# A four-layer graph network on one core: a written-out order for layer 2, and attention heads on quarters of the TensorE array

## The chip, the cores and the metric

The kernel runs on one core of a Trainium2 chip. The metric is the device time of one execution in microseconds; the kernel before takes 2139.83 us, the median of three runs (2136.4 to 2140.26). A profiled execution takes longer, 2252.29 us, and all times that come from the profile are on that longer scale.

## The reference, cut to what matters

Four graph layers run one after the other on x (8 batches, 2048 nodes, 64 features) with one sparse adjacency matrix of 2048 x 2048. Each is followed by x = layernorm(x + layer(x)). The change touches layers 2 and 3:

```python
# layer 2
agg = einsum('ij,bjf->bif', A, x) / maximum(deg, 1)
out = relu(x @ W_self + b_self + agg @ W_neigh + b_neigh)
out = layernorm(out) * ln_gamma + ln_beta
# layer 3: 4 heads, then one more attention over their result
h    = einsum('bnc,hdc->bhnd', x, Wh)
attn = softmax(where(mask, einsum('...nd,...md->...nm', h, h), NEG))
z    = leaky_relu(concat_heads(attn @ h + bh))
h2   = z @ Wo.T
out2 = leaky_relu(softmax(mask(h2 @ h2.T)) @ h2 + bo); out = layernorm(out2) * gamma + beta
```

## The kernel before, in words

**Tiles.** Nodes come in 16 tiles of 128 (NT), batches in four pairs (NP): a pair's two batches of 64 features fill 128 partitions once transposed. Each node tile has three lists of 128 gathered neighbours (GS) for each of four groups of 32 nodes (NG); a gather is one indirect DMA on GpSimd's queue (`gather`, L186) that brings 128 rows of 2 KB. Layers 1 and 2 compute the first nine node tiles (DENSE) with the matrix ET, transposed and held in SBUF, and the other seven with gathered lists.

**Layer 2, preparation.** For every tile X is transposed (`transposed`, L108), multiplied with W_self and W_neigh (L747), the neighbour part written to the table ytab (L752) and split into three bf16 pieces Y (L753 to L759), the self part put into S (L754), and beta added to X (L760). The weights of the heads are prepared in the same stretch: for each of the four heads Wh and Wo are loaded as block diagonals of two copies (L659, L660), and G = Wh' x Wh, AT and WoT are made from them (L663 to L670), two heads sharing a buffer.

**Layer 2, sums.** 144 steps (9 tiles x 16 blocks) of three matmuls each (L828) add up the matrix tiles; between them, at fixed spacing, the 21 quads of the list tiles (`add_edges`, L814: eight instructions on four strips of 32 columns of the array) and their gathers. `finish` follows a tile's last sum: scaling by 1/deg and adding S (L779), Relu on ScalarE (L780), and, when both of a pair of tiles (`mates`) are there, two layer norms with a product with gamma and the residual between them (L786, L787). A layer norm is four statistics instructions a tile on VectorE (L137), twelve small VectorE instructions for the inverse square root (L123 to L143), and eight ScalarE instructions a tile, one to a batch (L151). Then Xo, the copy of X whose feature 0 is a one, goes to the table xtab (L793). Tile 0 also runs `first_nodes`: scores of its nodes with themselves, from which the shift of the exponent is written into G, and the four sides U of tile 0. The order on each engine is made by the tile framework's scheduler here: it may move instructions of one engine ahead of others.

**Layer 3, heads.** Scores of nodes n and m for head h are x_n' G x_m. For each node tile, four groups of nodes times two parts of lists make eight steps, and the order of every engine is the order in the program (`tc.manual_schedule`). A step has: gathers six steps ahead (`fetch`); four PE transposes of a gathered tile to xsT (`turn`, L890) and ScalarE's copy (L892); `score` (L905), which multiplies each pair's two halves on two row halves of the array with the side U, then exp on ScalarE (L908) and the edge mask on VectorE (L914); and `back` (L931), which adds up weighted rows in po, on two column halves. Every second step po is copied to o (L936), which frees its only buffer. Into these steps the table `beside` puts the work of the tiles before and after: `load_nodes` and `turn_nodes` (x of the next tile, from xtab, transposed, L681), `side` (U = G x, L687, four heads), `sums` (the rows of ones turned into columns through a DRAM table, L948, and inverted, L949), `through_w` (AT x o, L953, Leaky Relu on ScalarE and VectorE, L956, L957), `through_wo` (z x WoT, L962, scaled by the inverted sums, L964, added up on GpSimd, L968) and `pieces` (three bf16 pieces for the last attention, L983 to L988). The products of `side`, `through_w` and `through_wo` use the whole 128 x 128 array with block-diagonal weights, half of which are zeros; their results go to PSUM tiles pm of one bank, of which there are two (f3psm). The second attention (fifth) follows and is not touched.

Instructions go to five engines with a queue each; a semaphore wait at the head of a queue holds everything behind it on that engine.

Of the kernel before, what the change touches and what calls it, by code (L numbers as in the profile page):

```python
# [48 lines left out]
def kernel(ctx: ExitStack, tc: tile.TileContext, ins: dict, out: bass.AP):  # L49
# [590 lines left out]
    ps_m = early.enter_context(tc.tile_pool(name="f3psm", bufs=2, space=PSUM))  # L640
# [5 lines left out]
    for Xo in ones_x:  # L646
        nc.gpsimd.memset(Xo[:, :, 0:1], 1.0)

# [3 lines left out]
    for h in range(HN):  # L652
        wb = hp.tile([P, P], F32, name=f"wb{h % 2}")
        nc.gpsimd.memset(wb, 0.0)
        ob = hp.tile([P, P], F32, name=f"ob{h % 2}")
        nc.gpsimd.memset(ob, 0.0)
        for k in range(2):
            half = slice(k * D, (k + 1) * D)
            nc.sync.dma_start(wb[half, half], ins["L3_gnn_Wh"][h])  # L659
            nc.sync.dma_start(ob[half, half], ins["L3_gnn_Wo"][:, h * D:(h + 1) * D])  # L660
            nc.vector.tensor_scalar(wb[half, half], wb[half, half], wb[half, k * D:k * D + 1], None, op0=ALU.subtract)
        pg = misc([P, P])
        nc.tensor.matmul(pg, wb, wb, start=True, stop=True)  # L663
        nc.vector.tensor_copy(G[:, h], pg)
        pw = misc([P, P])
        nc.tensor.transpose(pw, wb, ident)
        nc.vector.tensor_copy(AT[:, h], pw)
        pw = misc([P, P])
        nc.tensor.transpose(pw, ob, ident)
        nc.vector.tensor_copy(WoT[:, h], pw)  # L670
        for k in range(2):
            nc.sync.dma_start(AT[k * D:k * D + 1, h, k * D:(k + 1) * D], ins["L3_gnn_bh"][h:h + 1, :])
    Us, xTs = {}, {}
    mean_row = f3w.tile([P, P], F32, name="mean_row")
    nc.vector.memset(mean_row, 1.0 / (B * P))
    shift = f3w.tile([P, 1], F32, name="shift")

    def turn_nodes(it, xi):
        px = misc([P, NP, P])
        for p in range(NP):  # L680
            nc.tensor.transpose(px[:, p], xi[:, p * P:(p + 1) * P], ident)  # L681
        xTs[it] = hp.tile([P, NP * P], F32, name="xT", bufs=2)
        nc.scalar.copy(xTs[it], px.rearrange("p a n -> p (a n)"))

    def side(it, h):
        pu = misc([P, NP, P])
        nc.tensor.matmul(pu, G[:, h], xTs[it], start=True, stop=True)  # L687
        if h == 0:
            Us[it] = hp.tile([P, NP, HN, P], F32, name="U", bufs=2)
        if h % 2:  # L690
            nc.vector.tensor_copy(Us[it][:, :, h], pu)
        else:
            nc.scalar.copy(Us[it][:, :, h], pu)

    def first_nodes(xi):

        turn_nodes(0, xi)
        self_ = hp.tile([P, HN], F32, name="self_")
        for h in range(HN):
            pu = misc([P, NP * P])  # L700
            nc.tensor.matmul(pu, G[:, h], xTs[0], start=True, stop=True)
            sq = hp.tile([P, NP * P], F32, name="sq")
            nc.vector.scalar_tensor_tensor(sq, pu, 1.0, xTs[0], op0=ALU.mult, op1=ALU.mult, accum_out=self_[:, h:h + 1])
        pm = misc([P, HN])
        nc.tensor.matmul(pm, mean_row, self_, start=True, stop=True)
        nc.vector.tensor_scalar(self_, pm, -1.0, LEVEL, op0=ALU.mult, op1=ALU.add)
        for h in range(HN):
            for k in range(2):
                row = slice(k * D, k * D + 1)
                nc.vector.tensor_copy(G[row, h, row], self_[row, h:h + 1])  # L710
        for h in range(HN):
            side(0, h)

    with ExitStack() as l2:
        wp = l2.enter_context(tc.tile_pool(name="l2w", bufs=1))
        wk = l2.enter_context(tc.tile_pool(name="l2k", bufs=2))

# [9 lines left out]
        b2 = rows("b2", ins["L2_gnn_ln_beta"], wp)  # L727
        r_deg = wp.tile([P, NT], F32, name="r_deg")
# [34 lines left out]
        pa = l2.enter_context(tc.tile_pool(name="l2pa", bufs=3, space=PSUM))  # L763
        sums, rss, selfs, shown = {}, {}, {}, []

        mates = [(0, 1), (2, 3), (4, 5), (6, 7), (8,), (15, 14), (13, 12), (11, 10), (9,)]
        mate = {t: m for m in mates for t in m}

        def bank(it):
            m = mate[it]  # L770
            if it == m[0]:
                sums[m] = pa.tile([P, 2, B, D], F32, name="pa")
            return sums[m][:, m.index(it)]

        def finish(it):
            m = mate[it]
            po = sums[m][:, m.index(it)]
            zf = po.rearrange("p b d -> p (b d)")
            nc.vector.scalar_tensor_tensor(zf, zf, r_deg[:, it:it + 1], S[:, it].rearrange("p b d -> p (b d)"), op0=ALU.mult, op1=ALU.add)  # L779
            nc.scalar.activation(zf, zf, AF.Relu)  # L780
            if it != m[-1]:
                return
            zs = [sums[m][:, k] for k in range(len(m))]
            layer_norm(zs, wk)
            for t, z in zip(m, zs):
                nc.vector.tensor_tensor(z, z, over(g2, [P, B, D]), ALU.mult)  # L786
                nc.vector.tensor_tensor(X[:, t], z, X[:, t], ALU.add)  # L787
            layer_norm([X[:, t] for t in m], wk)
            for t in m:
                Xo = ones_x[len(shown) % len(ones_x)]  # L790
                shown.append(t)
                nc.scalar.copy(Xo[:, :, 1:], X[:, t, :, 1:])
                nc.sync.dma_start(xtab[t * P:(t + 1) * P, :], Xo.rearrange("p b d -> p (b d)"))  # L793
                if t == 0:
                    first_nodes(Xo.rearrange("p b d -> p (b d)"))

        quads = [(it, s) for it in by_list for s in range(GS)]

# [7 lines left out]
        def add_edges(n):  # L806
            it, s = quads[n]
            if s == 0:
                selfs[it] = wk.tile([P, GS, P], F32, name="self_")
                nc.scalar.activation(selfs[it], Sel[:, it], AF.Copy)  # L810
                sums[it] = bank(it)
            for g in range(NG):
                nodes = slice(g * GN, (g + 1) * GN)
                nc.tensor.matmul(sums[it][nodes].rearrange("p b d -> p (b d)"), selfs[it][:, s, nodes], rss[n][g],  # L814
                                 start=(s == 0), stop=(s == GS - 1))
# [3 lines left out]
        fetch(0)  # L819
        fetch(1)  # L820
        steps = [(it, jt) for it in by_matrix for jt in range(NT)]
        LATE, EARLY = 18, 10
        n = 0
        for k, (it, jt) in enumerate(steps):
            if jt == 0:
                sums[it] = bank(it)
            for q in range(3):
                nc.tensor.matmul(sums[it].rearrange("p b d -> p (b d)"), ET[:, jt, it * P:(it + 1) * P],  # L828
                                 Y[:, jt, q].rearrange("p a n -> p (a n)"), start=(jt == 0 and q == 0), stop=(jt == NT - 1 and q == 2))
            if jt == NT - 1:  # L830
                finish(it)
            while n < len(quads) and n * (len(steps) - LATE - EARLY) <= (k - LATE) * len(quads):
                add_edges(n)
                fetch(n + 2)
                n += 1
# [22 lines left out]
    with early, ExitStack() as heads:  # L858
# [5 lines left out]
        os, xss, xsTs, ws, pos, h2s, zs, dTs = ({} for _ in range(8))  # L864

        def load_nodes(it):
            xi = wk.tile([P, BD], F32, name="xi")
# [884 lines left out]
```

## Time and profile before

| what | from the profile of the kernel before |
|---|---|
| whole span | 2250.5 us, mean granted TensorE clock 0.775 |
| busy over the span | PE 1637.6, DVE 1390.5, ACT 997.3, POOL 1050.1 us |
| adjacency and layer 0 | 0 to about 530 us |
| layer 1 | to about 786 us |
| layer 2, preparation | 786 to 844 us |
| layer 2, sums and finishes | 844 to 1075 us, the first `turn` of the heads being at 1075.3 |
| heads | first steps to 1094, then evenly to 1785 us, last tile to about 1812 |
| second attention and checks | the rest |

PE is TensorE's matmuls, PEld its weight loads, DVE VectorE, ACT ScalarE, POOL GpSimd, SP the queue of the sync engine. Matmuls overlap in their pipeline, so a matmul's duration is longer than the time that it adds to a stream; that is read from the starts, or from the length of a run of them in the chain of waits. A float32 matmul appears as two instructions. The chain of waits follows the work back from the last instruction, at each step to what released it. The columns of a group are: line, engine, operation, what is written from what, shapes, count, busy us and mean ns of one, then the idle time just before it and what ended it.

### The profile page before, as it was taken

What the parts mean: (1) busy time and instruction counts of PE and PEld (TensorE: products, weight loads), DVE (VectorE), ACT (ScalarE), POOL (GpSimd) and SP (SyncE); (2) the same over time, 40 slices, a digit from 0 to 9 for tenths busy, and PEclk for the clock granted to TensorE, in tenths of its full rate; (3) what the DMA queues carried; (4) which work ended last, traced back from release to release, by engine and by line L of the source; (5) the groups of instructions that cost most, each with busy time, mean ns of one, the idle gap of its engine ahead of it and who ended that gap; (6) DMA issues with size and microseconds to landing.
All of it is one profiled execution on the core that took longest, in us unless ns stands there. A gap on an engine that the chain in (4) does not pass through costs nothing.

```text
span 2250.5 us, 33253 instructions
## 1 busy us (share of the span) xinstructions
PE 1637.6 (73%) x12259; PEld 909.4 (40%) x12294; DVE 1390.5 (62%) x2954; ACT 997.3 (44%) x2352; POOL 1050.1 (47%) x992
## 2 busy tenths in 40 slices
PE   3552445433899979862799998999899858878872
PEld 3541111111333363320677776777667612222220
DVE  6886587785655572435244444444444459999995
ACT  4542243438523252546344444444444324555555
POOL 0002666643645356430444444444434267777762
PEclk9855565566999999986799999999999955555555
DMA  7322666631278626441432233223322155555540
GB/s 196 134 98 82 180 183 182 182 112 57 94 264 301 221 85 177 131 123 42 123 93 81 85 101 103 74 89 101 106 70 84 54 155 161 151 157 161 160 135 21
DMA packets 127690, 287.47 MB, mean 128 GB/s; under 512 B 55680, under 2 KB 56192, under 8 KB 125440
## 3 DMA queue, kind: packets, MB, share of 16 engines
q0 software_dynamic: 64896, 217.10, 31.9%
q1 hardware_dynamic: 45984, 63.96, 8.5%
q10 hardware_dynamic: 16640, 4.20, 0.8%
q8 instruction: 99, 1.62, 0.3%
q14 instruction: 71, 0.58, 0.1%
HBM read 249.29 MB, written 35.91 MB: 127 GB/s over the span
## 4 chain that ended last, share of the span: by engine, by line
PE 39%; DVE 15%; ACT 7%; issue 7%; POOL 3%; DMA 2%; another core or an unknown queue 1%; SPq 0%; DVEq 0%; ACTq 0%; POOLq 0%
PE pscore L905 7%; PE pa L556 6%; PE po L931 5%; PE pt L890 5%; PE pm L953 3%; DVE pr L1078 3%; PE pa L828 3%; PE pm L687 2%; PE pm L962 2%; DVE w L914 2%; PE pa L608 2%; DVE st L137 2%; DVE sc L1083 2%; POOL hs L186 1%; ACT w L908 1%
## 5 line engine op out<-in xcount | busy, mean ns | idle before, releaser
L914 DVE SCALAR_TENSOR_TENSOR w<-w,Sel 128x512 f32<-128x512 f32 (+1 forms) x192 | 178.4, 956 | 257.9 <-ACT w L908 257.9
L186 POOL DMA_INDIRECT hs<-htab,src x192 | 183.8, 957 | 295.0 <-PE pe L408 203.7
L186 POOL DMA_INDIRECT xs<-xtab,src x192 | 200.1, 1042 | 133.5 <-DMA xtab<-Xo 63.4
L556 PE MATMUL pa<-R,ET 128*128 128x512 bf16 x841 | 197.0, 388 | 52.5 <-POOL R L544 34.2
L905 PEld LDWEIGHTS pscore<-U,xsT 64*128 64x128 f32 x3072 | 193.9, 198 | 82.2 <-issue 82.1
L151 ACT ACTIVATE X<-X,ln_m,ln_r 128x64 f32<-128x64 f32 x384 | 131.3, 427 | 204.2 <-DVE ln_m L143 75.0
L905 PE MATMUL pscore<-U,xsT 64*128 64x64 f32 (+1 forms) x3072 | 216.4, 290 | 0.0
L908 ACT ACTIVATE w<-pscore 128x1024 f32<-128x1024 f32 x128 | 131.0, 1024 | 191.0 <-PE pscore L905 126.2
L186 POOL DMA_INDIRECT hs<-ktab,src x192 | 186.3, 970 | 55.0 <-issue 47.7
L968 POOL TENSOR_TENSOR h<-h,h2h 128x512 f32<-128x512 f32 x48 | 60.9, 1269 | 270.8 <-DVE h2h L964 270.8
L1073 PE MATMUL pe<-hi,selTb 32*128 32x512 bf16 x576 | 138.8, 619 | 52.2 <-DVE pr L1078 27.9
L890 PE MATMUL pt<-ident,xs 128*128 128x128 f32 x768 | 132.7, 298 | 44.9 <-DMA xs<-xtab,src 37.1
L892 ACT COPY xsT<-pt 128x512 f32<-128x512 f32 x192 | 112.1, 584 | 117.5 <-PE pt L890 110.7
L931 PE MATMUL po<-w,xs 128*64 128x64 f32 (+1 forms) x3072 | 147.1, 246 | 17.6 <-DVE o L936 16.5
L556 PEld LDWEIGHTS <-ET 128*128 128x128 fp8e4 x864 | 84.4, 100 | 173.9 <-issue 82.7
L931 PEld LDWEIGHTS po<-w,xs 128*64 128x64 f32 x3072 | 122.0, 140 | 35.5 <-DVE o L936 18.7
L1078 DVE TENSOR_TENSOR pr<-pe,hs 128x1024 f32<-128x1024 f32 x96 | 116.9, 1217 | 15.0 <-DMA hs<-ktab,src 10.7
L186 POOL DMA_INDIRECT rs<-ytab,src x84 | 80.4, 957 | 82.6 <-PE pa L814 52.6
L1083 DVE TENSOR_REDUCE sc<-pr 128x16 f32<-128x1024 f32 x96 | 117.1, 1219 | 2.9
L828 PE MATMUL pa<-Y,ET 128*128 128x512 bf16 x420 | 102.0, 395 | 22.5 <-DVE X L787 12.6
L890 PEld LDWEIGHTS pt<-ident,xs 128*128 128x128 f32 x768 | 85.1, 147 | 72.5 <-issue 51.7
L1085 ACT ACTIVATE w<-sc,shift 128x16 f32<-128x16 f32 x96 | 29.3, 306 | 191.3 <-DVE sc L1083 146.5
(567 smaller groups left out, 3331.9 us busy)
## 6 DMA issues: line engine op xcount, KB each, us to landing
at<-in_adj SPq DMA_DIRECT2D x16, 1024.0 KB
rtab<-r SPq DMA_DIRECT2D x16, 512.0 KB
ptab<-hp SPq DMA_DIRECT2D x16, 384.0 KB
hi<-ptab SPq DMA_DIRECT2D x16, 384.0 KB
X<-in_x ACTq DMA_DIRECT2D x16, 256.0 KB
htab<-H SPq DMA_DIRECT2D x16, 256.0 KB
ytab<-y SPq DMA_DIRECT2D x16, 256.0 KB
xtab<-Xo SPq DMA_DIRECT2D x16, 256.0 KB
```

The costliest lines, as they stand in the source:

```text
L151: nc.scalar.activation(v[:, b], v[:, b], AF.Identity, scale=rstd[:, k:k + 1], bias=nmr[:, k:k + 1])
L186: nc.gpsimd.indirect_dma_start(out=dst, out_offset=None, in_=table[:, :], in_offset=bass.IndirectOffsetOnAxis(ap=src[:, it, s, g:g + 1], a ...
L556: nc.tensor.matmul(po[h].rearrange("p a f -> p (a f)"), ET[:, jt, it * P:(it + 1) * P], R[:, jt, q, h].rearrange("p a f -> p (a f)"), star ...
L828: nc.tensor.matmul(sums[it].rearrange("p b d -> p (b d)"), ET[:, jt, it * P:(it + 1) * P], Y[:, jt, q].rearrange("p a n -> p (a n)"), star ...
L890: nc.tensor.transpose(pt[:, p], xss[k][n][:, p * P:(p + 1) * P], ident)
L905: nc.tensor.matmul(pscore[:, k_, f0:f0 + HN * ni].rearrange("p (h i) -> p h i", i=ni), xsTs[k][t][half, p], Us[it][half, p, :, i0:i0 + ni] ...
L908: nc.scalar.activation(w.rearrange("p t k a h i -> p k t (a h i)"), pscore.rearrange("p k (t m) -> p k t m", t=n), AF.Exp)
L914: nc.vector.scalar_tensor_tensor(wt, wt, 3.0e38, edge, op0=ALU.min, op1=ALU.mult)
L931: nc.tensor.matmul(po[half, p, :, i0:i0 + ni], xss[k][t][:, f0:f0 + D], ws[k][:, t, k_, p], start=(s == 0 and p == 0), stop=(last and p == ...
L1073: nc.tensor.matmul(pe[:, k].rearrange("p b d -> p (b d)"), selTb[nodes, s * P:(s + 1) * P], hi[nodes, q], start=(q == 0), stop=(q == 2))
L1078: nc.vector.tensor_tensor(pr.rearrange("p k b d -> p (k b d)"), pes[u].rearrange("p k b d -> p (k b d)"), hss[u].rearrange("p k b d -> p ( ...
L1083: nc.vector.tensor_reduce(sc, pr, AX.X, ALU.add)
```

## The change

Four things are changed. In layer 2 the preparation of the heads' weights is moved out of the stretch ahead of the sums into it, as are the transposes of tile 0 and its scores (`beside` at steps 2 to 14, 64, 72 to 96 and 104), and the whole part is put under `tc.manual_schedule`, so that each engine's order is the program's. The finishes are gathered in batches of 2, 4, 4, 3, 1, 1 and 1 tiles in the order in which they end; Relu and the sum go to S in SBUF by VectorE, so that the PSUM sum is free after one instruction; the scaled z stands in two PSUM tiles of its own, and there are four sum tiles.

In the heads the products with G and with AT are made on four 64 x 64 quarters of the array, each with one non-zero block and two pairs of batches (`quarters`), so that no zeros are multiplied. Two of the quarters write to the other half of the partitions, so in pairs 2 and 3 the two batches change places; the table xtab holds these batches exchanged (three writes a tile), and `sums` and `through_wo` put them back. `through_wo` multiplies each half of z on its own row half with 64 columns instead of 128. The PSUM tile pm has two banks, one for each half, and there is one of it. `beside` gives at most one such product to each of two slots in a step, one ahead of the scores and one ahead of `back`. And x of the next tile comes from X in SBUF, with its rows of ones set by two memsets, instead of from the table.

```diff
+    def turn_nodes(it):
+        px = misc([P, NP, P])
+        for p in range(NP):
+            nc.tensor.transpose(px[:, p], X[:, it, 2 * p:2 * p + 2, :].rearrange("p b d -> p (b d)"), ident)
+        xTs[it] = hp.tile([P, NP * P], F32, name="xT", bufs=2)
+        nc.scalar.copy(xTs[it], px.rearrange("p a n -> p (a n)"))
+        for k in range(2):
+            nc.vector.memset(xTs[it][k * D:k * D + 1], 1.0)
...
-        pa = l2.enter_context(tc.tile_pool(name="l2pa", bufs=3, space=PSUM))
+        pa = l2.enter_context(tc.tile_pool(name="l2pa", bufs=4, space=PSUM))
+        pz = l2.enter_context(tc.tile_pool(name="l2pz", bufs=2, space=PSUM))
...
-        mates = [(0, 1), (2, 3), (4, 5), (6, 7), (8,), (15, 14), (13, 12), (11, 10), (9,)]
+        sizes = [2, 4, 4, 3, 1, 1, 1]
...
+            nc.vector.scalar_tensor_tensor(sf, sums.pop(it), r_deg[:, it:it + 1], sf, op0=ALU.mult, op1=ALU.add)
+            nc.vector.tensor_scalar(sf, sf, 0.0, None, op0=ALU.max)
...
+                pair_of = xtab[t * P:(t + 1) * P, BD // 2:].rearrange("n (a k d) -> n a k d", k=2, d=D)
+                for k_ in range(2):
+                    nc.sync.dma_start(pair_of[:, :, 1 - k_], Xo[:, B // 2 + k_::2])
...
+        beside = {**{2 + 4 * h: (prepare, h) for h in range(HN)}, 64: (turn_nodes, 0),
+                  **{72 + 8 * h: (own_scores, h) for h in range(HN)}, 104: (set_shifts,)}
...
+        with tc.manual_schedule(engines=engines):
+            fetch(0)
+            fetch(1)
...
+        ps_m = heads.enter_context(tc.tile_pool(name="f3psm", bufs=1, space=PSUM))
...
+            pq = misc2()
+            for k in range(2):
+                own = slice(k * D, (k + 1) * D)
+                for j in range(2):
+                    to = own if j == 0 else slice((1 - k) * D, (2 - k) * D)
+                    nc.tensor.matmul(pq[to, j, 0:2 * P], W[own, own], v[own, 2 * j:2 * j + 2].rearrange("p a n -> p (a n)"),
+                                     start=True, stop=True)
...
-                nc.tensor.matmul(ph[:, p], zs[it, h][:, p], WoT[:, h], start=True, stop=True)
+                for k in range(2):
+                    own = slice(k * D, (k + 1) * D)
+                    nc.tensor.matmul(ph[:, k, p * D:(p + 1) * D], zs[it, h][own, p], WoT[own, h, own], start=True, stop=True)
...
-            0: lambda it: [(load_nodes, it + 1)],
-            1: lambda it: [(through_w, it - 1, 0), (side, it + 1, 0)],
-            2: lambda it: [(sums, it - 1), (through_wo, it - 1, 0), (through_w, it - 1, 1)],
-            3: lambda it: [(through_wo, it - 1, 1), (through_w, it - 1, 2)],
-            4: lambda it: [(through_wo, it - 1, 2), (through_w, it - 1, 3)],
-            5: lambda it: [(through_wo, it - 1, 3), (side, it + 1, 1)],
-            6: lambda it: [(side, it + 1, 2), (side, it + 1, 3)],
-            7: lambda it: [(pieces, it - 1)],
+            0: lambda it: ([(turn_nodes, it + 1)], [(through_w, it - 1, 0)]),
+            1: lambda it: ([(side, it + 1, 0)], [(through_w, it - 1, 1)]),
+            2: lambda it: ([(sums, it - 1)], [(through_wo, it - 1, 0)]),
+            3: lambda it: ([(through_w, it - 1, 2)], [(through_wo, it - 1, 1)]),
+            4: lambda it: ([(side, it + 1, 1)], [(through_w, it - 1, 3)]),
+            5: lambda it: ([(through_wo, it - 1, 2)], [(side, it + 1, 2)]),
+            6: lambda it: ([(through_wo, it - 1, 3)], [(side, it + 1, 3)]),
+            7: lambda it: ([(pieces, it - 1)], []),
```

## The prediction

> **What bounds the kernel now.** I read the busy time of each engine stage by stage, then, for the two stages that the change touches, the groups by form, the chain of waits, the waits summed, and the timeline of one node tile. Columns of the first view: stretch, its length, busy us and instructions of PE, weight loads, VectorE, ScalarE, GpSimd, then granted clock and DMA.
>
> ```profile
> core 0: us, PE busy (x) PEld busy (x) DVE busy (x) ACT busy (x) POOL busy (x), PEclk, DMA share, GB/s
> 790.00:844.00 54.00, 44.21 (x209) 35.13 (x211) 41.57 (x90) 31.37 (x64) 30.12 (x36) 0.92 0.24 87
> 844.00:1070.00 226.00, 153.91 (x610) 53.22 (x619) 92.16 (x411) 109.49 (x297) 81.50 (x85) 0.84 0.39 118
> ...
> 1094.00:1785.00 691.00, 637.18 (x7587) 491.28 (x7585) 328.75 (x432) 307.22 (x450) 302.63 (x266) 0.96 0.29 88
> ```
>
> Layer 2 is bound by nothing: PE 154 of 226 us, no other engine over half. It waits on chains. The heads are PE's: 637 of 691 us. Of PE's work there (duration is from start to end, overlapped):
>
> ```profile
> L953 PE MATMUL pm<-o,AT 128*128 128x512 f32 x120 | 69.5, 663 | 33.9 <-DVE recs L949 33.9
> L962 PE MATMUL pm<-WoT,z 128*128 128x128 f32 x480 | 67.7, 281 | 0.7 <-issue 0.3
> L687 PE MATMUL pm<-xT,G 128*128 128x512 f32 x120 | 59.8, 601 | 0.0
> ```
>
> What an instruction costs in a stream is read from the chain (start, length, count). G (L687) takes 0.43 us an instruction, two to a product; four column strips at once (L814) 0.116 us an instruction of the same 512 columns; scores on two row halves 60 ns at 64 columns and 68 ns at 128, so there the columns don't set the pace.
>
> ```profile
> 1002.36 1.85 PE pa L814 x16
> ...
> 1243.10 1.93 PE pscore L905 x32
> 1246.64 1.72 PE pm L687 x4
> 1248.36 1.09 PE pscore L905 x16
> ```
>
> The same place in the chain (DVE w L914 of 1.75 us) recurs at 1166.31 and, twelve tiles later, at 1709.80: 45.3 us a tile. The summed waits (total, times, longest) and the timeline show two that come once a tile: an exp that starts late beside the row-sum transpose, and behind it W's product, which needs the buffer that the reciprocals free. The wait of 2.7 us is followed by PE at half pace: 2.08 us for the W pair that elsewhere takes 1.02.
>
> ```profile
> ACT w L908 <- PE pm L948: 46.7, 12, 3.9
> PE pm L953 <- DVE recs L949: 33.9, 14, 2.9
> 1270.41 2.08 PE L953 MATMUL pm<-o,AT 128*128 128x512 f32 x2 [2.74 <-DVE recs L949]
> 1272.41 2.08 PE L905 MATMUL pscore<-U,xsT 64*128 64x128 f32 x16
> ```
>
> For layer 2's end the chain shows the pieces of a finish: stats, a Newton chain of small VectorE steps, eight ScalarE steps.
>
> ```profile
> 1018.00 3.94 ACT pa L151 x13
> ...
> 1025.95 1.57 DVE st L137 x8
> 1030.99 1.48 ACT X L151 x5
> ...
> 1068.95 1.96 DMA xtab<-Xo
> ...
> 1075.33 1.10 PE pt L890 x4
> ```
>
> From these: eight scalings into PSUM 2.4 us (0.30 each), eight in X 2.65 (0.33), stats 0.8 a tile, Newton 3.5 (1027.5 to 1030.99), and 6.4 us from the last Xo copy (end 1068.9) to the first turn at 1075.3.
>
> **The Trainium skill.** *TensorEngine Tiling*, "Tiling Modes": 64x64 gives four independent tiles; "Changing tiling mode (not just tile) drains the TensorE". The trace shows two halves and four strips at once, not four 64x64 quarters; a drain is seen as some 0.1 us (turn before score 0.5, before G 0.39). *TensorE: Matmul & The Clock Gate*, "LDWEIGHTS": the load takes as long as it has columns, whatever the contraction; the 60 against 68 ns agree. The same page, Part 1: an idle PE falls to half clock; the timeline agrees. Its table of queues: ScalarE and VectorE are strict FIFO, so a fixed order is the order of waiting.
>
> **The change, part by part, in profiled time.**
>
> *Prologue (786 to 843.6).* 16 loads of Wh and Wo, some 0.6 us each on the sync queue, stand ahead of Wsn and of the layer's beta; the first product waits for Wsn until 795.7 and VectorE for beta until 805.9. In the new order Wsn goes out eight loads earlier (5 us), and G's, W's and Wo's preparation moves into layer 2. PE needs 16 x (0.43 + 1.95) = 38 us from about 791: end near 833. Gain 10 (6 to 12).
>
> *Layer 2.* PE: 144 steps x 0.648 + 21 quads x 0.99 = 114 us; Relu goes from ScalarE to VectorE, four more PSUM buffers let accumulations run ahead of a blocked finish, batches [2,4,4,3,1,1,1] share Newton chains. But the order is now program order. A batch of m costs, from its last sum: 2.0 (add, max, stats) + 3.5 + 2.4m (z) + 2.1 + 3.5, then 3.2m on ScalarE. Count from the first L828. Batch 2 closes at step 63: 64 x 0.648 + 8 x 0.99 = 49.4; z ends 64.6, X 83. Node tile 0's transpose copy stands behind it on ScalarE, its two memsets follow, and own_scores(0) at step 72 needs it: PE, there at about 57, waits until 84, some 27 us. Steps to 95 with 4 quads and 3 own scores: 22 us, 107 with the restart. Batch 3 then holds VectorE for 20.8; own_scores(3) is behind it and set_shifts' product (step 104) behind that: PE waits 14 us, to 129. Step 112 at 138; batch 4 holds VectorE until 156.5, ScalarE until 166. Then tiles 7, 9 and 8, each alone: X ends at 177, 191, 204. The table takes 6.4 + 1.2 (three writes in place of one) more: first turn at 212, before 231.7. Gain 20. Gathers (84 of 1.26 us from one to the next, 106 us) and writes lie beside this; so do the four sides of tile 0, which move into the wait for the table.
>
> *Heads, PE work of a tile.* Kept: 12 turns x 0.49, scores 4 x 1.93 + 4 x 1.09, back 4 x 1.08 + 4 x 1.02, transposing x 0.5, sums 0.2: 27.1. Through Wo: 8 instructions with 128 weight columns each are 16 now, in pairs; a pair loads 128 columns on each half, as scores do: 8 x 0.12 = 0.96 against 0.9. Nothing is gained. G and W: 8 products of 0.86 + 0.1; on quarters 256 columns, 2 x 0.21 if four run at once, + 0.15 for drain and loads: 0.57. The lower bound of the saving is zero or less (one after the other), the upper 0.43 each. I take four at once, as the strips do: 8 x 0.57 = 4.6. Sum 27.1 + 3.6 + 4.6 = 35.3.
>
> *Heads, waits.* Before: 45.3 less 38 of work = 7. Gone: the recs wait (2.7) and the half-paced stretch after it (2), as one misc product now comes at each of two slots in a step; and most of the 0.1 to 0.4 us at second turns, for the slot hides the copy. Added: misc holds two banks, one buffer. A W product is freed by Relu (0.6) and VectorE (0.7) behind that step's exp (1.02) and copy (0.59) on ScalarE and its mask (1.2) on VectorE. For example, counted from a tile's start: W 0 ends on PE at 3.1, ScalarE's exp and copy at 3.8, Relu at 4.4, VectorE's mask at 4.5, the product is free at 5.2, and side 0 is due at 4.7. Going through the eight steps so I get waits of 0.5 (side 0), 1.1 (sums), 0.1, 0.8 (side 1), 0.5 (Wo 2) and 0.5 (next tile's scores for the last U): 3.5, and I add 1 for late signals to ScalarE, which I can't explain: 40. The two memsets (1 us), two more reciprocals and exchanged reads lie on VectorE, half idle; the 15 loads of xi go, their time was hidden; the exchanged batches are an order of columns and cost nothing here. Gain 15 x 5.2 = 78. Last tile: one buffer in series, but W no longer behind the sums: 4.
>
> Sum 10 + 20 + 78 + 4 = 112 profiled. The profiled run is 2252.29 against 2139.83: x 0.95 = 106. 2140 - 106 = 2034, say 2035.
>
> **The rivals.**
> (1) Layer 2's order costs PE nothing (copies come sooner than I count) and the tile takes 38.3: 10 + 55 + 105 + 4 = 174, x 0.95: 1975. For: nothing but ScalarE's order makes those 41 us of PE waits, and without them I count 35 less at the end. Against: the instruction order puts that copy behind four X's.
> (2) New waits replace the old: the single buffer and the late signal keep a tile at 43 and half clock, layer 2 gains 10: 10 + 10 + 34 + 4 = 58, x 0.95: 2085. For: the late exp stands beside sums, which remain.
> (3) Slower: quarters run one after the other, 8 x 0.21 = 1.7 in place of 0.86: +6.7 a tile less 3 of removed waits, x 15 = +56; layer 2 loses the 10 that the prologue gains; x 0.95: 2140 + 53 = 2193. Against: strips and halves do overlap.
>
> **How the numbers follow.** Forecast 0.58, (1) 0.15, (2) 0.22, (3) 0.05. Range 1970 to 2090: it holds the forecast with its bounds, (1) and most of (2). Faster 0.93; same 0.02 (the lower edge of (2)); slower 0.05.
>
> **What would show it.** First L828 near 833; PE idle for 15 us or more at own_scores(0) behind the xT copy and again at set_shifts; first turn some 30 us earlier; L919's eight instructions in about 0.5 us with starts a few ns apart; through Wo at 0.9 us as before; a tile of 40 us with no half-clock stretch. Wrong if quarters start 0.2 us apart, if a misc wait passes 2.5 us and the clock falls, or if layer 2's PE waits are absent.

## The result, and the profile after

The kernel after takes 2152.02 us (median of four runs, 2148.22 to 2154.84) against 2140.05 us for the kernel before (2136.4 to 2142.82): a ratio of 1.0056, with a 95% interval of 1.0031 to 1.008. It is a little slower, by some 12 us. The forecast was 2035, with a range from 1970 to 2090.

One thing has to be said ahead of every number below. Chips come in two kinds here. The same kernel before takes 2140 us on the first kind (2136 to 2143) and 2241 to 2243 on the second (medians of two chips; 2235 to 2250 in all), two chips of each in the experiments; the times of the result are from the first kind, and the profile of before that the prediction read, with its 2252.29 us, fits the second. One stretch that the change leaves alone tells them apart in every trace: the products at L432 in layer 0 take 238 to 242 us from first to last in the eight traces of the first kind, 266 to 267 in the eight others of the experiments, and 269.1 in that first profile. It is not the profiler that takes the 110 us: on the first kind a profiled execution of the kernel before took 2141.39 us and one of the kernel after 2154.42. So the kernel before was profiled again on the first kind (the first experiment), and "before" below means that profile, unless the second kind is named. Kernels are compared with each other on one kind only.

Three stretches of the kernel after, on the first kind (preparation of layer 2, layer 2, heads), with the columns of the prediction's first view:

```profile
core 0: us, PE busy (x) PEld busy (x) DVE busy (x) ACT busy (x) POOL busy (x), PEclk, DMA share, GB/s
759.00:817.00 58.00, 40.97 (x194) 33.11 (x192) 41.76 (x76) 31.43 (x63) 30.95 (x43) 0.94 0.23 80
817.00:1047.00 230.00, 137.66 (x649) 51.96 (x662) 109.46 (x400) 108.37 (x280) 84.24 (x88) 0.79 0.40 116
1060.00:1687.00 627.00, 577.05 (x8835) 464.58 (x8835) 339.04 (x491) 303.91 (x450) 321.00 (x268) 1.00 0.31 93
```

The same stretches of the kernel before, on the first kind:

```profile
758.00:816.00 58.00, 44.70 (x208) 35.53 (x208) 44.36 (x94) 31.08 (x63) 29.81 (x40) 0.91 0.22 78
816.00:1031.00 215.00, 148.66 (x610) 52.33 (x622) 91.95 (x412) 109.83 (x297) 85.24 (x89) 0.87 0.42 128
1043.00:1678.00 635.00, 611.86 (x7642) 476.02 (x7641) 330.56 (x434) 309.83 (x451) 305.47 (x269) 1.00 0.33 98
```

The heads' PE is busy 35 us less, as the quarters promise, but the stretch is only 8 us shorter: PE stood still for 23 us of it before and for 50 after. Layer 2 is 15 us longer with 11 us less of PE work in it: PE stands still for 92 us and not 66. Read more closely, from the first and last starts and ends in the traces:

| stretch, us | before, second kind (read for the prediction) | before, first kind | after, first kind | after, second kind |
|---|---|---|---|---|
| layer 1's last product to layer 2's first | 57.6 | 58.9 | 58.0 | 60.4 |
| layer 2's first product to the first turn | 231.7 | 214.5 | 230.2 | 232.6 |
| first turn to first back | 18.5 | 12.4 | 13.0 | 18.5 |
| first back to last back | 693.8 | 634.6 | 627.0 | 670.3 |
| one tile of the heads, mean of 13 | 45.0 | 40.81 | 40.37 | 43.2 |
| last back to the second attention | 32.5 | 30.9 | 35.3 | 35.1 |
| span | 2250.5 | 2139.5 | 2152.5 | 2230.9 |

On the first kind: 15.7 lost in layer 2, 0.6 at the first steps, 4.4 behind the last tile; 7.6 won in the heads and 0.9 ahead of layer 2. That is 12.2 of the 13.0 us between the spans. The 0.9 is not safe: in the five other traces of the first kind with the same preparation that first row is 60.4 to 61.9. (The last column's execution was 10 us below the median there; times on that kind spread more, 2229 to 2252.)

What a product now costs on PE, in the groups by form of the kernel after (the G and W products, Wo, the row sums):

```profile
L1030 PE MATMUL pm<-WoT,z 64*128 64x64 f32 x976 | 67.8, 279 | 3.4 <-DVE z L1023 2.8 <-DVE recs L1016 0.6
L920 PE MATMUL pm<-o,AT 64*64 64x256 f32 x488 | 41.8, 413 | 15.7 <-DVE o L999 13.4 <-DVE z L1023 1.4 <-DVE h L1032 0.8
L920 PE MATMUL pm<-xT,G 64*64 64x256 f32 x440 | 36.4, 402 | 15.4 <-DVE z L1023 7.8 <-DVE h2h L1032 7.7
L1011 PE MATMUL pm<-ident,dT 32*128 32x32 f32 x15 | 3.7, 246 | 14.3 <-DVE z L1023 11.9 <-DMA dT<-dtab 2.4
```

An instruction's 0.4 us overlap with those of its neighbours; the chain of waits has the cost of a product. It also shows the period: the same VectorE step comes back after 40.29 us.

```profile
1229.94 1.29 DVE w L977 x2
...
1256.33 0.66 PE pm L920 x8
1256.99 1.96 PE pscore L968 x32
1258.97 1.03 ACT w L971
...
1266.60 0.59 PE pm L920 x8
1267.19 1.96 PE pscore L968 x32
1269.17 1.03 ACT w L971
1270.23 1.29 DVE w L977 x2
```

The quarters do overlap: eight instructions of 0.4 us in 0.59, 0.66 where PE had to wait first. And the exp (L971) follows its scores at once: there is no late start, and there was none before on this kind of chip either.

### The profile page after: what moved, and what is told of

It is laid out like the page before. It is cut to its first block, busy times and chain, and to the rows that moved or that the text cites. A ratio compares the mean times of both kernels' runs of the same rounds, so it can differ in the third digit from the quotient of the medians.

```text
span 2152.5 us, 35828 instructions
## 1 busy us (share of the span) xinstructions
PE 1554.6 (72%) x13538; PEld 879.8 (41%) x13574; DVE 1413.8 (66%) x2986; ACT 992.9 (46%) x2336; POOL 1068.2 (50%) x992
## 4 chain that ended last, share of the span: by engine, by line
PE 35%; DVE 18%; ACT 10%; issue 5%; POOL 2%; DMA 2%; SPq 1%; ACTq 0%; POOLq 0%; DVEq 0%
PE pscore L968 9%; PE pa L556 6%; DVE w L977 4%; PE pa L867 3%; ACT w L971 3%; PE pm L1030 3%; PE po L994 3%; PE pt L953 2%; DVE pr L1155 2%; ACT z L786 2%; PE pm L920 2%; PE pa L608 2%; PE po L1188 2%; ACT z L151 2%; DVE sc L1160 2%
## 5 line engine op out<-in xcount | busy, mean ns | idle before, releaser
L186 POOL DMA_INDIRECT xs<-xtab,src x192 | 205.4, 1070 | 123.0 <-issue 93.6
L971 ACT ACTIVATE w<-pscore 128x1024 f32<-128x1024 f32 x128 | 131.0, 1023 | 164.3 <-PE pscore L968 163.7
L968 PE MATMUL pscore<-U,xsT 64*128 64x64 f32 (+1 forms) x3072 | 203.6, 280 | 3.3 <-DVE U L931 3.3
L968 PEld LDWEIGHTS pscore<-U,xsT 64*128 64x128 f32 x3072 | 184.0, 190 | 29.0 <-issue 21.5
L151 ACT ACTIVATE X<-X,ln_m,ln_r 128x64 f32<-128x64 f32 x256 | 87.2, 428 | 172.0 <-DVE ln_m L143 172.0
L953 PE MATMUL pt<-ident,xs 128*128 128x128 f32 x768 | 128.1, 290 | 8.0 <-DMA xs<-xtab,src 5.4
L186 POOL DMA_INDIRECT rs<-rtab,src x84 | 79.6, 948 | 72.9 <-PE pa L608 52.8
L428 DVE TENSOR_TENSOR hs<-hs,w 128x2048 f32<-128x2048 f32 x48 | 106.7, 2277 | 0.5 <-ACT w L418 0.5
```

The lines of the kernel that those rows point to most:

```text
L151: nc.scalar.activation(v[:, b], v[:, b], AF.Identity, scale=rstd[:, k:k + 1], bias=nmr[:, k:k + 1])
L186: nc.gpsimd.indirect_dma_start(out=dst, out_offset=None, in_=table[:, :], in_offset=bass.IndirectOffsetOnAxis(ap=src[:, it, s, g:g + 1], a ...
L953: nc.tensor.transpose(pt[:, p], xss[k][n][:, p * P:(p + 1) * P], ident)
L968: nc.tensor.matmul(pscore[:, k_, f0:f0 + HN * ni].rearrange("p (h i) -> p h i", i=ni), xsTs[k][t][half, p], Us[it][half, p, :, i0:i0 + ni] ...
L971: nc.scalar.activation(w.rearrange("p t k a h i -> p k t (a h i)"), pscore.rearrange("p k (t m) -> p k t m", t=n), AF.Exp)
```

## The experiments

Two theories stood at the start. Theory 1: the profile of before is not a picture of the timed run; timed, a tile took some 40 us already, so the heads win little, and layer 2 loses a little. Theory 2: the heads do win the 70 us that the first pair of profiles shows, and the fixed order of layer 2 loses as much. Nothing of the computation is left out in any of the kernels. Which kind of chip a run falls on can't be chosen, so each result names it. Where a run fell on the second kind and its expectation names times near 2140, the ratio or the difference is what can be compared.

**Which profile is the timed run?** The kernel before again, and the kernel after again; no edit, nothing left out.

> The kernel before, unchanged, profiled once more. Its first profile had a span of 2250.5 us against 2140 us timed, and in it PE's completion signals came late in bursts. Theory 1 (that one profiled run was stretched; the timed run is not): the span is now near 2140, layer 0's stage at line 432 takes about 239 us as in the kernel after and not 269, and twelve node tiles of the heads take 38 to 40 us each and not 45.3. Theory 2 (the kernel before is truly slow in the heads, and quicker elsewhere than its profile shows): the span is near 2250 again or, if near 2140, the tile still takes 43 us or more.

> The kernel after, unchanged, beside the edits of the same call, since chips differ: the kernel before took 2140 us on one and 2243 us on another. On a chip of the first kind: 2152, a tile of 40.4 us. On one of the second kind: theory 1 (there, signals of PE's ends come late, before the change and after it, so the heads gain little there too): a tile of 43.5 to 44 us against 45.0 before, and 2236 to 2243, between same and 0.3% faster. Rival (the change does away with the late signals, as the first pair of profiles suggested): a tile of 40.4, 2180 to 2190.

The kernel before, on the first kind: 2141.39 us. The stage at L432 takes 239.8 us, as theory 1 had it; a tile takes 40.81, a little over its 38 to 40. In its chain of waits the step that marked a tile of 45.3 us in the prediction comes back after 40.80:

```profile
1113.64 1.75 DVE w L914
...
1154.44 1.76 DVE w L914
```

and PE's waits in the heads (total us, times, longest) are only these two; the wait for the reciprocals, 33.9 us in the prediction's view, is 6.7:

```profile
PE po L931 <- DVE o L936: 16.5, 15, 1.5
PE pm L953 <- DVE recs L949: 6.7, 15, 0.4
```

The kernel after, on the second kind: 2242.84 us against 2240.95 for the kernel before there, ratio 1.0004 (0.9991 to 1.0018). The change is no gain there either. In the heads the kinds differ in how long an exp on ScalarE waits after the end of the score products that it reads, taken from the starts and ends of 96 steps in the even part of the heads:

```
kernel, kind of chip    median us   steps over 1 us late   excess over the median, us   latest
before, second          0.11        12 of 96               29.7                         2.62
before, first           0.10         0 of 96                0                           0.62
after,  second          0.10         9 of 96               12.9                         1.97
after,  first           0.10         0 of 96                0                           0.29
```

In the chain of the kernel after on the second kind it looks like this: the exp begins at 1264.65, while the last score instruction began at 1262.98 and takes 0.3.

```profile
1260.39 1.70 PE pscore L968 x26
1262.98 1.65 PE pscore L968
1264.65 1.03 ACT w L971
```

On the second kind PE's ends reach ScalarE late, at a fixed place: all late exps, in all nine traces of that kind, belong to the third of a tile's eight steps. The Trainium skill warns, in *Perfetto Trace Analysis*, "Tensor Engine Instruction (MATMUL, LD_WEIGHTS)", that PE's end in a trace is modelled and that the semaphore's way lies behind it; the exp's start, though, is not modelled, and on the first kind it follows by 0.1 us. Nor is it ScalarE that is slow: the trace also has the times of PE's semaphore. In the kernel before on the second kind the scores of one such step end at 1264.60, that semaphore does not move between 1262.68 and 1267.12 and then moves four times within 0.25 us, and the exp starts 0.02 us after the first of these; in every late step of the nine traces it follows the semaphore as closely. VectorE's starts behind PE are not late in the same way (at most 0.3 us for U, the reciprocals and the products of Wo in the kernel after there, and 0.9 for one copy of po).

In all, a tile is 4.2 us longer on the second kind before the change (45.0 less 40.81) and 2.8 after (43.2 less 40.37). The late exps by themselves are 2.5 and 1.1 us of it (29.7 and 12.9 us over 12 tiles). In the kernel after ScalarE's copies to xsT, which also wait for PE, start over 1 us late at two more places of each of these tiles; and the granted clock is 0.96 in the heads instead of 1.00, before and after. How much each of these costs was not taken apart. Theory 1 held, for both kernels.

**Layer 2 alone, heads alone.** Two mixed kernels. e1 has layer 2 and its preparation from the kernel before, in the scheduler's order, with the edits below so that the heads of the kernel after can follow. e2 has everything up to the heads from the kernel after, with the first of these edits the other way round, and the heads of the kernel before. In both, the sides of tile 0 stand at the head of the heads.

```diff
-                nc.sync.dma_start(xtab[t * P:(t + 1) * P, :], Xo.rearrange("p b d -> p (b d)"))
+                nc.sync.dma_start(xtab[t * P:(t + 1) * P, 0:BD // 2], Xo[:, 0:B // 2].rearrange("p b d -> p (b d)"))
+                pair_of = xtab[t * P:(t + 1) * P, BD // 2:].rearrange("n (a k d) -> n a k d", k=2, d=D)
+                for k_ in range(2):
+                    nc.sync.dma_start(pair_of[:, :, 1 - k_], Xo[:, B // 2 + k_::2])
...
-        for h in range(HN):
-            side(0, h)
```

> Layer 2 and its preparation as in the kernel before (the scheduler orders them), the heads as in the kernel after: quarters for G and W, halves for Wo, the single two-bank misc buffer, the two slots, the exchanged table. Theory 1 (timed, the heads of before take 38 to 40 us a tile already, as their profile was stretched): within 15 us of the kernel before, 2130 to 2150. Theory 2 (the heads do gain the 70 us that the profiles show, and layer 2's fixed order loses as much): 2060 to 2075.

> Layer 2 in the fixed order, as in the kernel after, and the heads as in the kernel before (whole-array products, two one-bank misc buffers, node tiles read back from an unexchanged table); only the four sides of node tile 0 stand at the head of the heads. Theory 1: layer 2 moves the time little, 2130 to 2155. Theory 2: layer 2's fixed order loses 70 to 85 us, 2210 to 2225.

Heads alone: 2135.27 us against 2140.28, ratio 0.9981 (0.9972 to 0.999); layer 2 then runs from its first product to the last copy for the table in 204.5 us (before 208.2), and a tile takes 40.37. Layer 2 alone: 2158.64, ratio 1.0089 (1.0075 to 1.0103); 222.4 us, and a tile of 40.82. So the parts are -5.0 and +18.4, and their sum, 13.4, is close to the result, 12.0. Layer 2's fixed order is what loses, by far less than theory 2 had it (18 and not 70 to 85) and by 4 more than theory 1's band; the heads win next to nothing: 7 us in their even part, of which 5 are lost behind the last tile.

**What the quarters and the halves are worth.** Each is undone alone in the kernel after: first the quarters (with them go the exchanged table and the exchanged reciprocals), then the halves (the product then needs one bank).

```diff
-            for k in range(2):
-                own = slice(k * D, (k + 1) * D)
-                for j in range(2):
-                    to = own if j == 0 else slice((1 - k) * D, (2 - k) * D)
-                    nc.tensor.matmul(pq[to, j, 0:2 * P], W[own, own], v[own, 2 * j:2 * j + 2].rearrange("p a n -> p (a n)"),
-                                     start=True, stop=True)
-            return pq[:, :, 0:2 * P]
+            nc.tensor.matmul(pq[:, 0], W, v.rearrange("p a n -> p (a n)"), start=True, stop=True)
+            return pq[:, 0]
```

```diff
-                for k in range(2):
-                    own = slice(k * D, (k + 1) * D)
-                    nc.tensor.matmul(ph[:, k, p * D:(p + 1) * D], zs[it, h][own, p], WoT[own, h, own], start=True, stop=True)
+                nc.tensor.matmul(ph[:, p], zs[it, h][:, p], WoT[:, h], start=True, stop=True)
```

> The kernel after with the quarters alone undone: G's and W's products run on the whole array (two instructions of 0.43 us in place of eight that overlap in 0.59), so nothing is exchanged in the table and the reciprocals are one instruction; the single two-bank buffer and the slots stay. Theory 1, quarters save PE work that is on the path: 8 x 0.37 us a tile over 16 tiles, 40 to 50 us slower than the kernel after, 2195 to 2200. Rival: PE waits for the single buffer anyway, so the saving is hidden: 2152 to 2165.

> The kernel after, with the halves of Wo alone undone: eight instructions on the whole array in place of sixteen on two halves, one bank of the buffer used. By the starts on PE a product of Wo takes 0.89 us whole and 0.97 in halves. Theory (PE's own pace): 4 x 0.08 a tile, 5 us faster than the kernel after, 2145 to 2149. Rival (it is the wait in front, not the product, that sets the pace there): within 2 us, 2150 to 2154.

Without the quarters, on the first kind: 2185.25 us, 33 more than the kernel after, and a tile of 42.32. The groups of that kernel:

```profile
L911 PE MATMUL pm<-o,AT 128*128 128x512 f32 x116 | 62.0, 617 | 15.6 <-ACT xsT L945 13.6 <-DVE o L989 1.5 <-ACT w L961 0.6
L911 PE MATMUL pm<-xT,G 128*128 128x512 f32 x110 | 60.5, 632 | 9.8 <-DVE h2h L1020 7.7 <-DVE z L1011 2.2
```

So the quarters are worth 1.95 us a tile, of 2.9 that they take off PE's work (eight products at 0.59 in place of 0.95, by the starts). It lies below the 40 to 50 us that theory 1 gave and far above the rival: a third of the saving becomes waiting, for PE idles 2.3 us a tile without the quarters and 3.2 with them. The other edits in the heads (one buffer, slots, halves, x from SBUF) lose 1.5 us a tile, most of what the quarters win: 42.32 without the quarters against 40.81 before.

The halves of Wo: on the second kind the kernel after with a whole-array Wo took 2236.76 us (0.9967 of before, 0.9959 to 0.9976), some 6 to 8 us less than the kernel after there. The size that was expected, 5 us, was right, but not its reason. The 0.89 us of a whole-array product was read where another whole-array product followed. In the slots it is followed by scores or by `back`, and there, on the first kind, it takes 0.99 to 1.09 us, against 0.94 to 1.04 in halves: PE's own work is no shorter. And on the first kind a tile is no shorter either: 38.55 us with whole-array Wo in the last kernel below, 38.52 with halves and otherwise the same heads (medians of 13 tiles). Why the second kind gains is open.

**The single buffer.** PE's waits in the heads of the kernel after:

```profile
PE pm L1011 <- DVE z L1023: 12.8, 15, 0.9
PE pm L920 <- DVE o L999: 12.3, 14, 1.2
PE pm L920 <- DVE z L1023: 7.9, 14, 0.6
PE pm L920 <- DVE h2h L1032: 7.7, 14, 0.5
PE pscore L968 <- DVE U L931: 3.3, 15, 0.7
PE pm L1030 <- DVE z L1023: 2.8, 15, 0.2
```

A product on quarters occupies two banks: the Trainium skill says in *TensorEngine Tiling (Array Packing)*, "Restrictions and Gotchas", that row tiles write to different banks and cannot use one bank at once; no run here tried one bank. The kernel keeps a single pm of two banks for this, and W's product holds it longest: ScalarE reads it, then VectorE reads it again (z, L1023). The edit lets one engine read it:

```diff
-            nc.scalar.activation(zf, pn, AF.Relu, scale=0.8)
-            nc.vector.scalar_tensor_tensor(zf, pn, 0.2, zf, op0=ALU.mult, op1=ALU.add)
+            nc.scalar.copy(zf, pn)
+            nc.vector.scalar_tensor_tensor(zf, zf, 0.2, zf, op0=ALU.mult, op1=ALU.max)
```

> The kernel after, with W's product read out of its buffer by ScalarE alone: a copy to z, and VectorE makes the leaky Relu as the larger of 0.2 z and z, in place of Relu on ScalarE and a VectorE step that reads the product again. The result is the same function; the buffer comes free one VectorE step (0.68 us, behind the mask) sooner. Theory 1 (the single two-bank buffer costs PE 3.3 us a tile, and the releases by z at line 1023 are 2.3 us of it): 1 to 1.6 us a tile, 15 to 25 us faster than the kernel after, 2127 to 2137. Rival (PE's waits move to ScalarE's copy and to the chain beside it): within 5 us, 2147 to 2157.

> The kernel after with W's product read by ScalarE alone (a copy; the leaky Relu is then made by VectorE out of z in SBUF), once more, now beside the kernel after on the same chip. Theory 1 (VectorE's second read holds the single buffer, 1 to 1.6 us a tile): 15 to 25 us faster than the kernel after. Rival: within 5 us of it.

> The kernel after with W's product read by ScalarE alone. On a chip where the kernel before takes 2140: the waits at line 1011 and at the quarters behind z (2.3 us a tile together) shrink, a tile of 38.6 to 39.3 us against 40.37, 2127 to 2137. Rival (there PE's waits move to another release): a tile over 40, over 2146. On a chip of the second kind: about 18 us below the kernel after, as before.

On the second kind 2224.53 us (0.9921 of before) and, beside the kernel after on one chip, 2224.25 against 2242.84: 19 us. On the first kind 2126.12 us, 0.9942 of before (0.9928 to 0.9956), 26 us below the kernel after, and a tile of 38.64. PE's waits there: those for z are gone, the others are nearly as they were.

```profile
PE pm L920 <- DVE o L999: 12.9, 14, 1.2
PE pm L920 <- DVE h2h L1032: 7.7, 14, 0.6
PE pm L1011 <- DMA dT<-dtab: 3.5, 1, 3.5
PE pscore L968 <- DVE U L931: 3.4, 15, 0.7
```

The waits for z were 1.6 us a tile (23.5 over 15), the tile is 1.73 shorter: the single buffer's wait is on the path, close to one for one. The time is 1 us under the expected 2127 to 2137.

**The order of layer 2.** PE's waits in layer 2 of the kernel after: the side of tile 0 at the end, the own scores behind the transpose's copy, the shifts.

```profile
PE pm L920 <- DVE X L811: 36.9, 1, 36.9
PE pm L700 <- DVE xT L660: 28.8, 1, 28.8
PE pm L705 <- DVE pm L701: 15.6, 1, 15.6
```

The chain shows why: ScalarE scales the second batch (eight pieces of 0.44 a tile), then its four X, and only then copies xT.

```profile
877.63 0.42 ACT z L786
878.07 0.42 ACT z L786
878.51 0.42 ACT z L786
...
896.49 2.77 ACT X L786 x8
899.80 2.76 ACT X L786 x8
903.11 2.76 ACT X L786 x8
906.41 2.76 ACT X L786 x8
911.71 2.04 PE pm L700 x2
```

The edit puts tile 0's work ahead of that batch; the second run also finishes the last three tiles together.

```diff
-        beside = {**{2 + 4 * h: (prepare, h) for h in range(HN)}, 64: (turn_nodes, 0),
-                  **{72 + 8 * h: (own_scores, h) for h in range(HN)}, 104: (set_shifts,)}
+        beside = {**{2 + 4 * h: (prepare, h) for h in range(HN)}, 54: (turn_nodes, 0),
+                  **{57 + h: (own_scores, h) for h in range(HN)}, 62: (set_shifts,)}
```

```diff
-        sizes = [2, 4, 4, 3, 1, 1, 1]
+        sizes = [2, 4, 4, 3, 3]
```

> The kernel after, with one change in layer 2's written order: node tile 0's transposes at step 54 and not 64, its own scores at steps 57 to 60 and not 72 to 96, the shifts at step 62 and not 104, all ahead of the close of the second batch (step 63). Nothing is left out. Theory 1 (the fixed order loses because PE waits some 29 us for the transpose's copy behind the batch's four X on ScalarE and 16 us at the shifts, and the batches behind close later for it): those two waits are gone, the third batch closes some 28 us sooner, layer 2 ends 25 to 35 us sooner, 2118 to 2128. Rival (the finishes' chain on VectorE and ScalarE sets layer 2's end whatever PE does): under 8 us, 2144 to 2152.

> The kernel after with the transposes, own scores and shifts of node tile 0 ahead of the second batch's close, once more. On a chip where the kernel before takes 2140: if those waits are what layer 2 loses, it ends 20 us or more sooner than in the kernel after (208 us or less from its first product to its last copy for the table, against 223), and the time is 2125 to 2132. If the loss there is in the finishes: over 2144. On a chip of the second kind: about 28 us below the kernel after, as before.

> As the run before it, and the last three node tiles finish as one batch: sizes 2, 4, 4, 3, 3 and not 2, 4, 4, 3, 1, 1, 1. A tile alone costs 12.7 us in series at the end of layer 2, three in a batch 13 + 3.3 x 3 for the scalings of z and 3.3 x 3 for X. Theory (the singles are in series and the chain sets the end): 8 to 14 us less than with the singles, 2108 to 2118. Rival (the batch must wait for the last tile's sum, step 143, so the singles had hidden their work beside PE): 0 to 8 us slower than with the singles.

With tile 0's work early, on the first kind: 2128.96 us, 0.9949 of before (0.9936 to 0.9962), 23 us below the kernel after; layer 2 runs from its first product to the last copy in 198.3 us against 223.0. PE's waits there:

```profile
PE pm L920 <- DVE X L811: 47.1, 1, 47.1
PE pa L847 <- DVE S L794: 6.7, 1, 6.7
...
PE pm L700 <- DVE xT L660: 2.8, 1, 2.8
```

Of 28.8 us at the own scores 2.8 are left, and the wait at the shifts is gone. PE is finished earlier and waits longer at the very end, 47 us: what is left ahead of the end is the finishes' chain. On the second kind 2215.06 us (0.9876 of before), 28 below the kernel after, and with the last tiles in one batch 2203.85 (0.9822): another 11 us less, inside the expected 8 to 14. The rival, that singles hide beside PE, fell; the batch shortens layer 2 by 14 us in the traces, so at its end the finishes' chain sets the pace.

**All of it.** Three of these edits together, then all four.

> The kernel after with three edits at once: own scores and shifts ahead of the second batch's close, batches 2, 4, 4, 3, 3, and W's product read by ScalarE alone. If they act on separate stretches (the first two on layer 2, 22 and 13 us by the profiles; the third on the heads, 15 to 25 us), they add up: 50 to 60 us faster than the kernel after on the same chip. Rival (the earlier table only moves the start, and gathers then hold up the heads): under 40 us.

> As the run before it, with Wo's products on the whole array. If PE's pace counts there: 4 x 0.08 us a tile, 4 to 6 us faster than with the halves; rival (the change of array mode, or one bank shared by all, costs as much): within 2 us.

> All edits: own scores early, batches 2, 4, 4, 3, 3, W read by ScalarE alone, Wo on the whole array. On a chip where the kernel before takes 2140: the sum of the parts below the kernel after, 20 + 12 + 20 + 5, so 2090 to 2102. On a chip of the second kind: about 61 us below the kernel after, as before.

Both layer-2 edits and W's one reader, on the second kind: 2188.11 us against 2242.84 for the kernel after, 55 less, in the expected 50 to 60. With the whole-array Wo: 2182.09, 6 less again, as on that kind before. The last kernel on the first kind: 2096.15 us (2092.02 to 2097.94), 0.9792 of before (0.9779 to 0.9805), 56 us below the kernel after, in the expected 2090 to 2102, though Wo gave nothing in its tiles: the two edits that were also timed alone on this kind gave 23 and 26 us, and the batches some 11 by the traces. It beats both kernels. Its layer 2 and heads:

```profile
816.00:1010.00 194.00, 135.22 (x649) 51.32 (x662) 102.70 (x353) 107.71 (x280) 84.47 (x89) 0.84 0.47 139
1023.00:1630.00 607.00, 581.79 (x8353) 470.35 (x8355) 338.65 (x491) 303.45 (x450) 317.03 (x268) 0.99 0.31 96
```

## Why the prediction was wrong

**The step that failed** is the base of the heads' sum: it took a tile of 45.3 us from the profile, put 7 us of it down to waits, counted 4.7 of these as removed, and at the end scaled everything by 0.95, as if the 110 us between profile and timed run were spread evenly. On the kind of chip that was timed a tile of the kernel before takes 40.81 us. The reciprocals' wait is 0.4 us a tile there and not 2.7, and the half-paced stretch is not there, so hardly anything of the 4.7 was there to remove. Gain 78, or 74 once scaled; measured, 7.6. Of the 118 us between forecast and result this is some 66; layer 2's order is some 35, the prologue and the last tile some 8 each.

The 110 us are not spread evenly: 29 are in layer 0's stage at L432 (269.1 us against 239.8), which the change leaves alone, 17 in layer 2 (231.7 against 214.5), 6 at the first steps and 59 in the heads (693.8 against 634.6). The preparation of layer 2 (57.6 against 58.9) and all from the second attention on (430 us in both) have none. In the heads the late ends of PE's products come with it; the other stretches were not taken apart. The prediction had seen the sign, "late signals to ScalarE, which I can't explain", and allowed 1 us a tile for it after the change. On the second kind a tile is 2.8 us longer than on the first; on the first kind none of the 96 exps is late, before or after.

**Bounds.** That PE bounds the heads and nothing bounds layer 2 holds on both kinds.

**Prologue, gain 10: it is 0.9 at best.** The first product with Wsn starts 9.8 and 9.7 us after layer 1's last product, before and after, and waits for Wsn last in both:

```profile
PE py L747 <- DMA Wsn<-in_L_gnn_W_neigh: 0.8, 1, 0.8
PE py L748 <- DMA Wsn<-in_L_gnn_W_neigh: 1.9, 1, 1.9
```

The prediction had 16 loads of Wh and Wo ahead of Wsn. The sync queue shows eight ahead of it before the change and eight behind it; the same eight still go first, so Wsn comes no sooner. Then the products wait for ScalarE's copies of the transposes, 7.3 us of the weight loads' time against 2.8, so that PE ends no sooner although it has less to do.

**Layer 2, first turn at +212, gain 20: it is +230.2, a loss of 15.7.** Both PE waits are where they were foretold, 28.8 and 15.6 us for 27 and 14. Two sizes were off. The second batch's close came 6 us late (55.4 after the first product, not 49.4). And a scaling of z was counted at 0.30 us an instruction; from S in SBUF into PSUM it takes 0.44, so 3.4 a tile and not 2.4, with 14 tiles of it on the chain by the prediction's own count. That is 20 us, an estimate, for 18 that are missing. The third error is again the base: 231.7 on the second kind, 214.5 where it was timed.

**Heads, PE work.** Quarters at 0.57 are 0.59 to 0.66; through Wo 0.96 is 0.94 to 1.04. The saving, counted as 38 less 35.3, or 2.7 a tile, is 2.2 by the busy time.

**Heads, waits.** The waits after the change were counted at 3.5 us and 1 for late signals, and are 3.2 by PE's idle time, 1.5 before it. A tile of 40 was foretold and is 40.37 (the mean of 13 tiles). In part that is luck: by the busy time PE's work is 37.2 us a tile and not 35.3, the waits are 3.2 and not 4.5, and the two errors cancel. The kernel before that it was compared with was another chip's.

**Last tile, gain 4: a loss of 4.4.** That one buffer in series costs more there than the order saves was not tested by itself; with one reader of W's product the stretch behind the last tile is 33.7 us, against 35.3 with two and 30.9 before.

**The rivals.** Nearest in its mechanism is (2), new waits in place of the old, but it kept 34 us in the heads and 10 in layer 2. The slower case (3) rested on quarters that run one after the other, and they don't. That the two parts might cancel at zero was none of the cases.

What stays open: why PE's ends come late on one kind of chip, and why at one step of a tile, and why layer 0 is longer there. Nor is it known whether it is the chip or a state that it keeps: each of the four chips was seen in one set of runs.

## What to carry to other kernels

Compare the profiled run with the timed ones before reading it. Where it is 5% longer, as here, the excess can sit in a few stages, and one factor for all is wrong; a wait that ends long after its producer should be taken for absent until a profile of a run with the timed length shows it. When a faster product needs twice the buffer, count who releases it: here most of the work saved on PE (1.7 of 2.2 us a tile) came back as waits; of the 3.2 us that PE then waited, 1.6 were for W's product with its two readers, and giving it one reader won 1.7 us a tile. A fixed order is only as good as the place of each small copy in it: one copy behind four long ones on ScalarE's queue stopped PE for 29 us, and ten steps earlier it cost 3.

## What the hardware showed beyond that

The same program takes 2140 us on two of the chips and 2241 to 2243 on two others, each within 0.4% of its median, with PE's semaphore up to 2.6 us late on the latter. ScalarE's scaling of 128x64 float32 starts every 0.33 us from SBUF to SBUF, every 0.41 from PSUM to PSUM (median; 0.29 at the least), and every 0.44 from SBUF to PSUM.
